# A graph kernel's edge search: gathers fetched a superblock ahead, the target list loaded alone

## The chip, the cores and the metric

The kernel runs on one core of one Trainium2 chip. The metric is device time in microseconds (us) of one execution; lower is better. The engines are named as in the profile: PE (TensorE, with PEld for its weight loads), DVE (VectorE), ACT (ScalarE), POOL (GpSimd) and SP (SyncE); a q behind a name is the engine's queue of DMA issues.

## The reference

A graph of N = 3125 nodes and E = 100,000 edges, sorted by target node `dst`, with a source `src` and one of 8 edge types. Node features `x` are 3125 x 128 in float32. Four layers follow one another, each added to its input and normalised over the features:

```python
x = _layernorm(x + gcn3(x, src, dst))                 # three GCN layers, 1/sqrt(degree) weights
x = _layernorm(x + sum_of_linear(x, src, dst))        # h[src] summed by dst, with self loops
x = _layernorm(x + gin(x, src, dst))                  # sum of neighbours, two batch norms
x = _layernorm(x + rgcn2(x, src, dst, edge_type_8))   # two layers, mean per type and target
```

Every sum over edges is a product with an adjacency matrix, in the last layer with one such matrix per edge type.

## The kernel before

The nodes are 25 blocks of 128 (`NB`), padded to 3200. The kernel first makes the dense adjacency matrix as counts, then multiplies with it. It is written in a tile framework: the program gives the operations, and a scheduler orders them on each engine when the kernel is built, adds the waits, and may bring a later operation forward into a gap. Each engine and each DMA queue then works in that order.

**Building** (`listed`, pool `f_t1`). The three edge lists are loaded as 125 x 800 (`ei`, L170). The targets are cast to float (`df`) and written back as `dsf`, 500 rows of 200. Every 200th target is loaded once more as the sample row `smp` (L173), spread over all partitions by a matmul (`smb`). Type, source and target are packed into one word per edge and stored as `pk` (L183 to L188). A superblock is 256 targets, two per partition; there are 13 (`SB`). `search(s)` counts the samples below each target (L212), gathers the row of 200 that it points to (`g`, L219, on POOL), counts in it (L224), and so has the first edge of each target (`ptr`). `keys(s)` gathers the next 64 words from there (`ew`, L234) and splits them into key columns, which PE transposes and ACT copies to `kT` (L255). `total(b)` makes block b in four units: one-hot matrices `lo` and `hi` of the keys on DVE (L161), 16 small matmuls (L271), and a cast on ACT into `at` (L273, two buffers). Then the identity is added on DVE (L277), `at` is stored as `adj_t` (L278), transposed on PE (L283), evicted by ACT to `av` (L284), stored as `adj` (L286), and summed over its rows with a column of ones (L290). The loop is

```python
search(0)
search(1)
keys(0)
for s in range(SB):
    if s + 2 < SB:
        search(s + 2)
    if s + 1 < SB:
        keys(s + 1)
    total(2 * s)
    if 2 * s + 1 < NB:
        total(2 * s + 1)
```

After it the row sums become `dinv` = 1/sqrt(degree): seven single-row copies into `rs` (L312), transposes (L314), square roots on ACT (L318 to L321), a reciprocal on DVE (L322). Sums over `at0` and `held` (L327 to L339) give the first edge of each block and a flag, `bad`.

**Layers.** With `f_t1` closed, the pool `f_nd` takes its memory. Weights, `xa` (the features) and bias rows are loaded on ACT's queue (L473 to L496). `v` = `xa` times `dinv` is split into three bfloat16 `parts` (L501 to L505), and `product` multiplies them with `adj`, read back as `m` (L514), in 525 matmuls per layer (L534); `done` applies the weight, the normalisation and the next split. Three GCN layers make 105 steps of 15 matmuls.

**The relations.** `relations` is a generator of work that `product` draws on: after each step `fill(1.3)` advances it 1.3 yields. It counts edges per type (L347, L348, eight times) into the reciprocals `inv`, gathers the edges of 11 blocks that are later treated edge by edge (`gedge`, L376), decodes them, and makes the per-type matrices of the 14 other blocks in 56 units: `rlo`, `rhq` (L161), L429, 16 matmuls (L448), casts (L455 on ACT, L457 on DVE), stores (L462). What follows, the other three layers, is not touched.

Of the kernel before, what the change touches and what calls it, by code (L numbers as in the profile page):

```python
# [8 lines left out]
F32 = mybir.dt.float32  # L9
# [63 lines left out]
def listed(ctx: ExitStack, tc: tile.TileContext, p: dict, out: bass.AP, bad):  # L73
# [11 lines left out]
    onesb = const.tile([P, 1], BF, name="onesb")  # L85
# [5 lines left out]

    def column(name, n=1):
        t = const.tile([P, n], F32, name=f"c_{name}")
        with nc.allow_non_contiguous_dma(reason="a bias"):
            nc.scalar.dma_start(t, p[name].rearrange("(n p) -> p n", p=P))
        return t
# [51 lines left out]
    with ExitStack() as lists, tc.tile_pool(name="f_ps", bufs=1, space=PSUM) as psum:  # L148
# [6 lines left out]
        begin = bg.tile([P, SB, 2], F32, name="begin")  # L155

# [9 lines left out]
        with tc.tile_pool(name="f_t1", bufs=1) as t1:  # L166

            ei = [t1.tile([EP, ET], I32, name=f"e_{n}") for n in ("dst", "src", "edge_type_8")]
            for t, name in zip(ei, ("dst", "src", "edge_type_8")):
                nc.sync.dma_start(t, p[name].rearrange("(p t) -> p t", p=EP))  # L170
            smp = t1.tile([1, 500], I32, name="smp")
            with nc.allow_non_contiguous_dma(reason="every 200th edge"):
                nc.scalar.dma_start(smp, p["dst"].rearrange("(o i j) -> o i j", o=1, j=200)[:, :, 0])  # L173
# [3 lines left out]
            smf = t1.tile([1, 500], F32, name="smf")  # L177
            nc.vector.tensor_copy(smf, smp)
            df = t1.tile([EP, ET], F32, name="df")
            nc.vector.tensor_copy(df, ei[0])  # L180
            nc.sync.dma_start(dsf.rearrange("(p a) c -> p (a c)", p=EP), df)
            w = t1.tile([EP, ET], I32, name="w0")
            nc.vector.scalar_tensor_tensor(w, ei[2], 12, ei[1], op0=OP.logical_shift_left, op1=OP.bitwise_or)  # L183
            w2 = t1.tile([EP, ET], I32, name="w1")
            nc.vector.scalar_tensor_tensor(w2, ei[0], 15, w, op0=OP.logical_shift_left, op1=OP.bitwise_or)
            none = t1.tile([GM, P], I32, name="none")
            nc.vector.memset(none, -1)
            nc.sync.dma_start(pk[:E].rearrange("(p t) o -> p (t o)", p=EP), w2)  # L188
            nc.sync.dma_start(pk[E:].rearrange("(o t) c -> o (t c)", o=GM), none)

            t = psum.tile([P, 512], F32, name="mi", tag="mi", bufs=2)
            nc.tensor.matmul(t[:, :500], ones[0:1, :], smf, start=True, stop=True)
            smb = t1.tile([P, 500], F32, name="smb")
            nc.scalar.copy(smb, t[:, :500])
# [101 lines left out]
            for s in range(SB):  # L296
                if s + 2 < SB:
                    search(s + 2)
# [1276 lines left out]
```

## Time and profile before

| | us |
|---|---|
| median of 3 runs | 2141.09 |
| lowest, highest | 2141.07, 2145.42 |
| the profiled execution | 2231.44 |
| its span, first to last instruction | 2229.5 |
| PE busy in it | 1911.2 (86%) |
| DVE busy in it | 1269.3 (57%) |
| ACT busy in it | 1056.7 (47%) |
| POOL busy in it | 900.9 (40%) |

The profile is of one execution, 4% longer than the median. The page cuts the span into 40 slices of 55.7 us and gives a digit for each, the busy share in tenths. Below, a row of a timeline has start and duration in us, engine, line, operation, output from inputs with shapes, and in brackets the idle time before it and what ended that. A row of waits has the waiting group, what it waited for, total us, number and longest. A row of windows has the stretch, its length, the busy time (and number of instructions) of PE, PEld, DVE, ACT and POOL, the clock granted to TensorE, the DMA share and GB/s.

### The profile page before, as it was taken

How to read it: one execution, taken by the hardware profiler on the slowest of the kernel's cores; microseconds unless marked ns; L12 is line 12 of the kernel's file. 1: busy time of each engine (PE TensorE's matmuls, PEld its weight loads, DVE VectorE, ACT ScalarE, POOL GpSimd, SP SyncE). 2: the span in 40 equal slices, each digit the busy share in tenths (PEclk: the TensorE clock that was granted, in tenths of full speed). 3: DMA queues.
4: the chain of work that ended last, by engine and by line, in shares of the span. 5: the costliest groups of instructions: out<-in, count | busy, mean ns of one | idle time of the engine just before them, and what ended most of it. 6: DMA issues, size and time to landing. Idle time of an engine off the chain costs nothing.

```text
span 2229.5 us, 31941 instructions
## 1 busy us (share of the span) xinstructions
PE 1911.2 (86%) x12176; PEld 1382.8 (62%) x12176; DVE 1269.3 (57%) x2303; ACT 1056.7 (47%) x1151; POOL 900.9 (40%) x898
## 2 busy tenths in 40 slices
PE   1767769999999699778998999898878998998984
PEld 0455536666665588556677667567636776777773
DVE  4888889999996563363444445344236443334333
ACT  1767744544442466542232333232327676766760
POOL 3222121221120000027657357437525766766664
PEclk9777779999999899988999999999989999999996
DMA  3444466888787788175656567446538877778762
GB/s 86 190 177 174 177 202 206 273 291 270 263 270 250 238 264 238 45 213 157 168 168 165 169 178 201 128 150 170 148 105 252 239 215 211 224 219 235 205 168 68
DMA packets 384636, 433.06 MB, mean 194 GB/s; under 512 B 28731, under 2 KB 350301, under 8 KB 384472
## 3 DMA queue, kind: packets, MB, share of 16 engines
q1 hardware_dynamic: 314318, 278.95, 40.8%
q0 software_dynamic: 45920, 119.66, 18.2%
q10 hardware_dynamic: 24234, 32.31, 5.0%
q8 instruction: 97, 1.59, 0.3%
q14 instruction: 67, 0.55, 0.1%
HBM read 319.22 MB, written 111.58 MB: 193 GB/s over the span
## 4 chain that ended last, share of the span: by engine, by line
PE 58%; DVE 17%; DMA 8%; issue 7%; ACT 4%; another core or an unknown queue 3%; POOL 2%; ACTq 0%; SPq 0%; DVEq 0%; POOLq 0%
PE acc L772 24%; PE ga L814 7%; PE acc L534 7%; PE acc L569 6%; PE mi L852 4%; PE mi L862 3%; DVE lo L161 2%; DMA g<-dsf,irow 2%; PE bld L448 2%; DVE rhq L161 2%; ACT m L767 2%; DVE hi L161 2%; DVE rlo L161 1%; DMA back<-ht_d 1%
## 5 line engine op out<-in xcount | busy, mean ns | idle before, releaser
L772 PE MATMUL acc<-m,hilo 128*128 128x384 f32 (+1 forms) x3200 | 776.2, 386 | 44.8 <-issue 28.6
L772 PEld LDWEIGHTS acc<-m,hilo 128*128 128x128 f32 x3200 | 580.4, 194 | 132.3 <-issue 53.1
L767 ACT CAST m<-m 128x2560 fp32r<-128x2560 uint8 (+1 forms) x224 | 454.7, 2061 | 438.2 <-remote 140.4
L806 POOL DMA_INDIRECT gx<-xt_d,gsrc x355 | 388.4, 1094 | 553.9 <-DMA inv<-inv_d 293.5
L806 POOL DMA_INDIRECT gx<-ht_d,gsrc x355 | 364.8, 1028 | 213.1 <-issue 77.5
L534 PE MATMUL acc<-m,parts 128*128 128x512 bf16 (+1 forms) x1575 | 333.7, 358 | 11.6 <-DMA r_L_gnn_g<-in_L_gnn_g 10.5
L814 PE MATMUL ga<-oh,gx 128*128 128x192 bf16 (+1 forms) x2442 | 264.7, 245 | 65.6 <-issue 38.1
L814 PEld LDWEIGHTS <-gx 128*128 128x128 bf16 x2442 | 178.7, 99 | 156.4 <-issue 126.5
L798 DVE TENSOR_TENSOR oh<-iota,gkey 128x768 bf16<-128x768 bf16 (+1 forms) x188 | 100.1, 533 | 263.9 <-PE ga L814 134.1
L534 PEld LDWEIGHTS <-parts 128*128 128x128 bf16 x1575 | 152.5, 98 | 135.2 <-issue 13.6
L769 DVE CAST m<-m 128x2560 fp32r<-128x2560 uint8 (+1 forms) x96 | 151.9, 1584 | 115.8 <-PE ga L814 32.2
L455 ACT CAST rb<-bld 128x800 uint16<-128x800 f32 x179 | 143.8, 829 | 124.3 <-PE bld L448 119.2
L462 POOL DMA_DIRECT2D rel<-rb x112 | 64.4, 583 | 285.3 <-ACT rb L455 181.2
L569 PE MATMUL acc<-mf,halves 128*128 128x512 f32 (+1 forms) x700 | 155.0, 379 | 16.9 <-ACT mf L566 16.7
L569 PEld LDWEIGHTS acc<-mf,halves 128*128 128x128 f32 x700 | 128.6, 191 | 37.5 <-issue 18.3
L161 DVE TENSOR_TENSOR lo<-iota,kT 128x2048 bf16<-128x2048 bf16 x100 | 121.7, 1217 | 0.0
L746 DVE TENSOR_TENSOR e<-mi,t 128x512 f32<-128x512 f32 x50 | 34.3, 687 | 137.5 <-ACT t L745 134.5
L566 ACT CAST mf<-m 128x2560 fp32r<-128x2560 bf16 (+1 forms) x42 | 88.2, 2102 | 47.9 <-PE acc L569 38.7
L271 PE MATMUL bld<-hi,lo 128*128 128x50 bf16 x1600 | 75.0, 201 | 40.0 <-DVE hi L161 24.2
L448 PE MATMUL bld<-rhq,rlo 128*128 128x200 bf16 x896 | 106.9, 252 | 1.6 <-DVE rb L457 1.0
L448 PEld LDWEIGHTS <-rlo 128*128 128x128 bf16 x896 | 82.5, 98 | 36.0 <-issue 7.6
L271 PEld LDWEIGHTS <-lo 128*128 128x128 bf16 x1600 | 64.1, 107 | 64.3 <-DVE hi L161 27.1
(230 smaller groups left out, 2093.2 us busy)
## 6 DMA issues: line engine op xcount, KB each, us to landing
m<-rel SPq DMA_DIRECT2D x160, 320.0 KB
rel<-rb POOLq DMA_DIRECT2D x112, 400.0 KB
m<-adj SPq DMA_DIRECT2D x60, 640.0 KB
m<-rel SPq DMA_DIRECT2D x160, 240.0 KB
m<-adj_t SPq DMA_DIRECT2D x40, 640.0 KB
m<-adj SPq DMA_DIRECT2D x45, 480.0 KB
adj_t<-at SPq DMA_DIRECT2D x25, 800.0 KB
adj<-av SPq DMA_DIRECT2D x25, 800.0 KB
```

The source lines that it names most:

```text
L161: nc.vector.tensor_tensor(o, (iota2 if of is None else of)[:, None, :width, :].to_broadcast([P, PU // 2, width, 2]), k[:, :, None, :].to_b ...
L271: nc.tensor.matmul(pt[:, j, : 2 * NB], lo[:, j // 2, :, j % 2], hi[:, j // 2, :, j % 2], start=True, stop=True)
L448: nc.tensor.matmul(pt[:, k, : R * NB], lo[:, j // 2, :, j % 2], hq[:, j // 2, :, j % 2], start=True, stop=True)
L455: nc.scalar.copy(o, src)
L534: nc.tensor.matmul(o, x[:, k, :], m(k - k0), start=(k == 0 and i == 0), stop=(k == NB - 1 and i == 2))
L569: nc.tensor.matmul(acc[:, :w], x[:, 5 * g + k, :], mf[:, k, :w], start=(g == 0 and k == 0 and i == 0), stop=(more is None and g == 4 and k ...
L767: nc.scalar.copy(v, src)
L769: nc.vector.tensor_copy(v, src)
L772: nc.tensor.matmul(acc[:, :w], x[:, 5 * g + k, :], m[:, k, :w], start=(g == 0 and k == 0 and i == 0), stop=(g == 4 and k == 4 and i == 1),)
L798: nc.vector.tensor_tensor(oh[:, : nt // 2], iota2[:, None, : GW * R, :].to_broadcast([P, nt // 2, GW * R, 2]), gkey[:, g, t : t + nt].rear ...
L806: nc.gpsimd.indirect_dma_start(out=gx.rearrange("p i c -> p (i c)"), out_offset=None, in_=table[:], in_offset=bass.IndirectOffsetOnAxis(ap ...
L814: nc.tensor.matmul(acc[:, a:z], gx[:, i, :], oh[:, t % 4 // 2, a - c0 : z - c0, t % 2], start=(a // 512 not in seen), stop=(t == GT[g] - 1 ...
```

## The change

- The target list is loaded first; the other two lists wait for it. The sample row is no longer loaded but made from `df`: four columns of it times the identity (`smf`), summed by a matmul with ones.
- The loads of `xa`, of all weights, rows and bias columns move from ACT's queue to SP's, wait for the store of the packed words (`later`), and, but for the columns and `xa`, lie in a pool of their own, `f_w`. The packing waits for the first superblock's coarse count.
- `search` is split: `coarse(s)` counts the samples and issues the gather of `g`; `search(s, gs)` counts in what came. `keys` is split likewise by `fetch_edges(s)`. The loop runs `coarse` three superblocks ahead, `search` and `fetch_edges` two, `keys` one.
- `total` is split: what follows the casts (`stored`) comes after the first two units of the next block.
- The row sums use a 32-column `onesb` and give 32 equal rows; three wide copies take the place of the seven single-row ones and of the clearing of `rs`, which has one buffer. An early square root on ACT brings its table in.
- `at0`, `held` and `bad` move into `relations`, followed by the gathers of `gedge`, which stood behind the counting; the counting gets a yield per type; the store of `inv_d` moves behind the decoding. `fill` has 1.4 for 1.3.

```diff
-    onesb = const.tile([P, 1], BF, name="onesb")
+    onesb = const.tile([P, 32], BF, name="onesb")
...
+    nc.scalar.activation(const.tile([P, 1], F32, name="root_eps"), eps_ln, AF.Sqrt)
+    packed = []
+    def later(ld):
+        tc.add_manual_dep(ld.ins, packed[0].ins.name, WAIT, reason="the edges come first")
...
-            nc.scalar.dma_start(t, p[name].rearrange("(n p) -> p n", p=P))
+            later(nc.sync.dma_start(t, p[name].rearrange("(n p) -> p n", p=P)))
...
+        def square(name):
+            t = wp.tile([D, D], F32, name=f"w_{name}")
+            later(nc.sync.dma_start(t, p[name]))
+            return t
+        def row(name):
+            t = wp.tile([P, D], F32, name=f"r_{name}")
+            later(nc.sync.dma_start(t, bcast(p[name], D)))
+            return t
...
+            for ld in loads[1:]:
+                tc.add_manual_dep(ld.ins, loads[0].ins.name, WAIT, reason="the targets come first")
...
-                nc.scalar.dma_start(smp, p["dst"].rearrange("(o i j) -> o i j", o=1, j=200)[:, :, 0])
...
+                for i in range(4):
+                    nc.vector.tensor_scalar(smf[:, :, i], ident[:EP, :EP], df[:, 200 * i : 200 * i + 1], None,
+                                            op0=OP.mult)
+                t = psum.tile([P, 512], F32, name="mi", tag="mi", bufs=2)
+                nc.tensor.matmul(t[:, :500], ones[:EP, :], smf.rearrange("p a i -> p (a i)"), start=True, stop=True)
+                nc.scalar.copy(smb, t[:, :500])
...
-            def search(s):
+            def coarse(s):
...
+                gs = []
                 for c in (2 * s, 2 * s + 1):
                     g = t1.tile([P, 200], F32, name="g", bufs=4)
                     nc.gpsimd.indirect_dma_start(
                         out=g, out_offset=None, in_=dsf[:],
                         in_offset=bass.IndirectOffsetOnAxis(ap=irow[:, c : c + 1], axis=0),
                     )
+                    gs.append(g)
+                return gs
+
+            def search(s, gs):
+                own = slice(2 * s, 2 * s + 2)
+                for c, g in zip((2 * s, 2 * s + 1), gs):
                     junk = t1.tile([P, 500], BF, name="junk", bufs=2)
                     nc.vector.tensor_scalar(junk[:, :200], g, nid[:, c : c + 1], 0.0, op0=OP.is_lt,
                                             op1=OP.add, accum_out=fine[:, c : c + 1])
...
-            def keys(s):
-                own = slice(2 * s, 2 * s + 2)
+            def fetch_edges(s):
                 ew = t1.tile([P, 2, SL], I32, name="ew", bufs=3)
...
+                return ew
+
+            def keys(s, ew):
+                own = slice(2 * s, 2 * s + 2)
...
-            def total(b):
+            def total(b, behind):
                 at = t1.tile([P, NB, P], BF, name="at", bufs=2)
                 for u in range(64 // PU):
+                    if u == 2 and behind is not None:
+                        stored(*behind)
...
+                return b, at
+
+            def stored(b, at):
                 nc.vector.tensor_add(at[:, b, :], at[:, b, :], identb)
                 nc.sync.dma_start(adj_t[b], at)
...
+            for s in range(-3, SB):
+                if s + 3 < SB:
+                    near[s + 3] = coarse(s + 3)
+                if 0 <= s + 2 < SB:
+                    search(s + 2, near.pop(s + 2))
+                    edges[s + 2] = fetch_edges(s + 2)
+                if 0 <= s + 1 < SB:
+                    keys(s + 1, edges.pop(s + 1))
+                for b in range(max(2 * s, 0), min(2 * s + 2, NB)):
+                    built = total(b, built)
+            stored(*built)
+
+            tc.add_manual_dep(words.ins, started[0].ins.name, WAIT, reason="the search comes first")
...
-                rs = t1.tile([P, 512], F32, name="rs", bufs=2)
-                nc.vector.memset(rs, 0.0)
-                for i in range(4 * g, min(7, 4 * g + 4)):
-                    q, w = 32 * (i % 4), min(512, NP - 512 * i)
-                    nc.scalar.copy(rs[q : q + 1, :w], row[g][q : q + 1, :w])
+                rs = t1.tile([P, 512], F32, name="rs")
+                if g == 0:
+                    nc.scalar.copy(rs, leave[0])
+                else:
+                    nc.scalar.copy(rs[:64], leave[1][:64])
+                    nc.scalar.copy(rs[64:96, :P], leave[1][64:96, :P])
...
-                        fill(1.3)
+                        fill(1.4)
```

## The prediction

> **What bounds the kernel now.** I read the page's 40 slices first. VectorE (DVE) is at 8 or 9 tenths in slices 1 to 11, the only stretch that the change touches apart from slice 0; after it TensorE (PE) leads.
>
> ```profile
> PE   1767769999999699778998999898878998998984
> DVE  4888889999996563363444445344236443334333
> ```
>
> Then the timeline gives four landmarks: first one-hot of the building stage (`lo`, L161) at 42.11 us, last one-hot (`hi`) ending at 285.04, TensorE running the layers' products (L534) without gaps from 312.96, and their end near 731. Before 42.11 the chain of waits is a row of transfers:
>
> ```profile
> 16.05 0.41 DVE L178 CAST smf<-smp 1x500 f32<-1x500 int32 x1 [13.28 <-DMA smp<-in_dst]
> ...
> 25.74 1.11 POOL L219 DMA_INDIRECT g<-dsf,irow  x1 [20.70 <-DMA dsf<-df]
> ...
> 42.11 1.22 DVE L161 TENSOR_TENSOR lo<-iota,kT 128x2048 bf16<-128x2048 bf16 x1
> ```
>
> The samples (`smp`) land at 16, the target list written back (`dsf`) at about 25.7, and the first gather needs both. For the building stage I took the busy times and the waits of DVE in that window, and one stretch at its end without gathers (columns: PE, weight load, DVE, ACT, POOL busy, then the granted clock, DMA share, GB/s):
>
> ```profile
> 42.10:285.10 243.00, 167.18 (x2372) 119.30 (x2373) 211.19 (x461) 165.65 (x302) 56.04 (x44) 0.77 0.45 172
> 333.00:690.00 357.00, 353.30 (x2338) 220.90 (x2337) 347.73 (x628) 172.12 (x249) 63.20 (x109) 1.00 0.80 264
> ```
> ```profile
> DVE junk L224 <- DMA g<-dsf,irow: 22.4, 15, 3.6
> DVE at L277 <- ACT at L273: 8.3, 19, 0.9
> ```
> ```profile
> 128.40:140.30 11.90, 7.53 (x108) 6.09 (x108) 11.72 (x20) 6.28 (x11) 2.99 (x2) 0.57 0.35 137
> 262.00:290.00 28.00, 20.01 (x361) 14.45 (x360) 26.78 (x44) 24.82 (x48) 0.00 (x0) 0.99 0.56 228
> ```
>
> DVE works 211.2 of 243 us; its 31.8 idle us are two waits: the search waits for its own gather (22.4), and the addition of the identity (L277) waits for ACT's last cast (8.3, and 0.9 unnamed). ACT (165.7) and PE (167.2) have room. So the stage is DVE plus two waits. Between the stages stands a third:
>
> ```profile
> 298.28 0.32 DVE L322 RECIPROCAL dinv<-dinv 128x25 f32<-128x25 f32 x1 [1.67 <-ACT dinv L321]
> ...
> 308.97 1.01 ACTq L485 DMA_DIRECT2D r_L_gnn_beta<-in_L_gnn_beta  x1
> ...
> 310.02 1.55 ACT L501 CAST parts<-v 128x512 bf16<-128x512 f32 x3 [11.57 <-DMA gedge<-pk,gi]
> ...
> 310.74 0.59 PE L534 MATMUL acc<-m,parts 128*128 128x512 bf16 x1 [10.49 <-DMA r_L_gnn_g<-in_L_gnn_g]
> ```
>
> The 11.57 us are put down to a gather, but ACT's own queue was issuing twelve weight and row loads from 298.97 to 309.98; the cast stands behind them.
>
> **What the Trainium skill says.** "DMA: Bandwidth & Descriptors", section Anatomy of one DMA, prices a transfer at about 2.0 us plus bytes over 436 GB/s. The gathers agree: issued at 34.22, used at 36.94. The write of `dsf` doesn't: 0.4 MB would be 2.9 us, and it took 7.9 (16.96 to 24.86) at a DMA share of about a third; the edge lists, too, have 125 rows. I use the trace. The same page, section Issuing engines are not separate DMA queues, says that moving a load to another issuer saves only sequencer time; here that time is the 11 us above. "ScalarE: Activation LUTs", section What ACT_TABLE_LOAD costs, gives 1283 ns; the trace has 1.28 us at L318. "TensorE: Matmul & The Clock Gate", section What's actually happening, says an idle window halves the clock: the trace has 0.57 at 128.4 to 140.3 and 0.99 at 262 to 290.
>
> **The change part by part.** Times as H, the end of the last `hi`.
>
> *Start.* The target list is loaded alone (the other two lists wait for it, `xa`, weights and rows wait for the packed words); `smp`, 500 separate elements, goes, and the samples come from `df` by four small DVE steps (0.2 us each by their size, near L178's row of 0.41), one matmul of 500 columns (2.03, row L192) and the copy (0.58). From 14 to 16 us, with `xa` mostly in, the core's transfers ran at 120 GB/s; I take that as the lists' own rate (an estimate), so one takes 3.4 us of transfer and lands near 6.2. Then 0.56 + 1.2 + 2.03 + 0.58 puts the samples at 10.7, and four coarse counts of 0.66 put the first rows at 13.6. `dsf` is issued near 7, but behind the two other lists (0.8 MB, 6.7 us at that rate) on SP's queue: 16 to 22; I take 19. So the first gather goes from 25.7 to 19. From there the order on POOL is four gathers, g2, two `ew`, g2, two `ew`; g2 waits for the search of superblock 1. At 1.25 us an issue and 2.7 to land (34.22 to 36.94): search 1 done at +7.2, last `ew` issued at +13.5, landed +16.2, keys of superblock 1 (1.7) before the first `lo`: +18, where it is +16.4 now. First `lo` at **37** instead of 42.1: -5. Bounds 31.5 (`dsf` in time for 13.7) and 41 (at 23).
>
> *SP's queue.* 26 loads now stand on SP between the packed words and the first `adj_t` store. They can be issued from some 25 us; 26 x 0.4 us (ACT's issues of them now: 0.33 to 0.97) plus the landing of 1.6 MB of `xa` (8 us at the 205 GB/s of 6 to 12 us; each load waits in the program for the eighth before it) ends before 45; the first store is due after six pairs of one-hots, 37 + 9.7 = 47. Cost nothing; if that cover is gone, it is ACT's third block that waits for the buffer.
>
> *Building.* `coarse` issues superblock s+3's gather before s+2 is searched, `fetch_edges` one iteration ahead of `keys`, and `stored` comes two pairs into the next block. Both DVE waits lose their cause. The counts stay, but the third coarse count, search 2 and keys 1 (4.4 us) are done before the first `lo`: 211.2 - 4.4 = 206.8. What is late next: the `at` buffer (two) is now stored half a block later, so ACT's first cast of block b+2 waits for the landing of b's store: issued, then four more pairs of DVE and PE work when no search lies between (6 us), against 800 KB, at the busy rate (3.2 MB in 45% of 20.2 us, 2.3 us each) plus 2 to 3: 4.3 to 6. And PE at the low clock needs per block 4 x 0.86 + 25 x 0.12 + 6.3 x 0.59 = 10.2 us, warm 4 x 0.58 + 25 x 0.07 + 6.3 x 0.38 = 6.5; DVE asks one per 8.5. Warm it fits; cold it would be busy throughout, and in 262 to 290 a busy share of 71% already goes with 0.99. I put 9 us (0.8 a superblock) for both, bounds 0 and 22. The 32-column `onesb` costs PE at most the difference of weight loads, 0.10 against 0.08 us, x175 = 3.5, beside DVE. H = 37 + 206.8 + 9 = 252.8 against 285.04: **-32**, the start included.
>
> *Between the stages.* Now H + 27.9 for gapless L534. The last casts and evictions (H + 6.4) stay. Seven one-row copies (6 x 0.59 + 0.26) become three (0.58, 0.58, 0.27), the table load (1.28) has moved to the idle start; a single `rs` gives some back: -2.5 at the reciprocal. `at0` and `held` leave the pool, so the first `m` load no longer waits for their matmul (6.4 us on SP). One `cnt` reduction (1.88) stays in front of `v` on DVE. Without the twelve loads ACT casts at once; the limit is now `m`: issued near H + 11, 640 KB in 4 us, H + 15; gapless two later: H + 17.5: **-10** (bounds -6, -12).
>
> *Layers.* PE is 99% busy, DVE 97%. The edge gathers (11 on POOL, 1.4 us each) move ahead of the counting; DVE waits 1.3 us for them at L381 now, so at most that is gained; POOL has nothing else due. `inv_d`'s store moves behind the decoding, needed hundreds of us later. The merged `iv` copy saves 0.4. The generator has ten more yields and rate 1.4: done after 128/1.4 = 91 steps of 105, as 118/1.3 now. But two counts (4.9 us) move into a full DVE, and in the new PE order the units lie between the 210th and 1380th L534 instead of 139th and 1365th: 56 x 0.19 = 11 us less PE cover for the same DVE work, against 9 of slack: **+4** (bounds -1, +15).
>
> Sum: -32 - 10 + 4 = **-38** on the profiled execution's 2231.44, so 2193; the median of the runs is 2141.09, 4% less, and the same ratio gives 2104. Extremes: -62 (2082) and -7 (2134).
>
> **The rivals.** (a) The forecast, all three gains, 0.74. (b) PE becomes the bound of building by staying at the low clock: 25 x 10.2 = 255, H = 292, total +7 - 10 + 4: 2232, **2142**, no change. For it: 0.77 now; against it: 0.99 at a PE share of 71% in 262 to 290. 0.04. (c) DVE starves PE in the layers by the whole 11 + 5 and a like amount from the normalisations queued behind the one-hots: +25, so -17, **2125**. For it, DVE's 97%; against it, 40 us of plain products after the last unit. 0.12. (d) Slower: ACT's first cast waits for the `adj_t` store. The loop over two blocks is landing time L plus 9.5 us of pairs, cast and addition; beyond L = 10.7 it is longer than 20.2, and from about 12 it eats the start and the -10 too; at L = 15 it is 24.5 x 12 = 294 instead of 243: +51 - 5 - 10 + 4 = +40, **2179**. For it, `dsf` at 7.9 us for half the bytes; against it, 128 rows and a share of 0.45. 0.06. (e) The loads' order doesn't change what lands when (the lists are as late): first `lo` at 42, -33, **2109**, inside (a). Left: 0.04 better than 2078.
>
> **The numbers.** The likeliest is 2104. Range 2078 to 2132: (a), (c) and (e) with the bounds of the terms. No change means within 0.2%, about what a measurement of this kernel can tell: 0.04; slower 0.06; faster 0.90.
>
> **What would show it.** First `lo` near 37 and the first gather near 19; no DVE wait on `g`; superblocks of 17.4 to 18.2 us where they are 20.2; ACT casting `parts` within 3 us of the reciprocal; gapless products 18 us after the last `hi`; from there to the end the same within 5 us. It is wrong if superblocks stay near 20, with ACT waiting for a store or PE's clock near 0.6, or if PE waits in the layers for one-hots.

## The result, and the profile after

The changed kernel takes 2126.75 us (median of 6 runs, 2122.28 to 2130.2), the kernel before 2144.95 beside it (6 runs). The ratio is 0.9915 (95% interval 0.9898 to 0.9933): 18 us faster, where 37 were forecast. Measured again with the experiments (c0 below) it was 0.9940 (0.9922 to 0.9959). So the direction was right and less than half of the gain came.

The profiled execution of the kernel before (2231.44) was 4% above its runs, that of the changed kernel (2126.84) is like its runs. The two traces can be compared up to the end of the layers, at some 730 us; the last section says what lies behind it.

The slices of the page show DVE full to slice 12 (53 us each, 56 before) and PE leading after it, so each stage is led by the same engine as before:

```profile
PE   1667689999999699967999999999888999999994
DVE  4999888999998464263535345525434544444432
```

Four landmarks from the timelines (first `lo`; H, the end of the last `hi`; the layers' products without gaps; end of the last product):

| | first `lo` | H | gapless products | last product |
|---|---|---|---|---|
| before | 42.11 | 285.04 | 312.96 | 729.96 |
| forecast | 37 | 252.8 | 270.3 | 691 |
| after | 47.07 | 271.05 | 287.82 | 710.43 |

By stage: start +5 (forecast -5), building 242.9 to 224.0, -19 (forecast -27), between the stages 27.9 to 16.8, -11 (forecast -10), layers 417.0 to 422.6, +5.6 (forecast +4). The sum is -19.5, about what the timed runs show. The start and the building stage are where 18 us are missing.

**Start.** The timeline of the changed kernel (start, duration, engine, line, operation, output and input, in brackets the idle time and what ended it):

```profile
19.36 1.11 POOL L259 DMA_INDIRECT g<-dsf,irow  x1 [14.32 <-DMA dsf<-df]
...
33.97 0.94 POOL L279 DMA_INDIRECT ew<-pk,ptr  x1 [0.30 <-DMA g<-dsf,irow]
...
35.22 0.94 POOL L279 DMA_INDIRECT ew<-pk,ptr  x1 [0.30 <-issue]
...
45.37 0.23 DVE L288 TENSOR_SCALAR f<-ew 128x128 int32<-128x128 int32 x1 [5.19 <-DMA ew<-pk,ptr]
...
47.07 1.22 DVE L183 TENSOR_TENSOR lo<-iota,kT 128x2048 bf16<-128x2048 bf16 x1
```

The first gather starts 0.4 us from its forecast. But the edges (`ew`) of superblock 1, issued at 33.97 and 35.22, are used at 45.37: ten microseconds to land, where 2.7 had been put down.

**Building.** The windows of the changed kernel for building and for the time to gapless products (columns as in the prediction), and then DVE's waits in the first of them:

```profile
47.07:271.05 223.98, 151.81 (x2381) 112.58 (x2381) 205.75 (x439) 160.31 (x299) 131.67 (x40) 0.82 0.48 185
271.05:287.82 16.77, 9.96 (x81) 5.60 (x78) 15.08 (x24) 10.90 (x27) 4.48 (x4) 0.78 0.68 241
```
```profile
DVE f L288 <- DMA ew<-pk,ptr: 12.5, 7, 3.5
DVE junk L270 <- DMA g<-dsf,irow: 5.7, 4, 3.2
```

DVE works 205.75 us (forecast 206.8) and waits 18.2, all of it for late gathers. POOL's 131.67 us are new: before, 56 us in a stage 19 us longer. The group on the page and one gather in the timeline tell why (g: 988 ns in the median before, 1887 at most):

```profile
L259 POOL DMA_INDIRECT g<-dsf,irow x26 | 78.1, 3003 | 79.3 <-DVE fine L272 51.5
```
```profile
81.54 14.28 POOL L259 DMA_INDIRECT g<-dsf,irow  x1 [0.30 <-issue]
81.68 1.22 DVE L183 TENSOR_TENSOR lo<-iota,kT 128x2048 bf16<-128x2048 bf16 x1
...
94.42 0.58 DVE L183 TENSOR_TENSOR hi<-iota,kT 128x800 bf16<-128x800 bf16 x1
94.90 0.73 DVE L251 TENSOR_SCALAR_CACHE_REDUCE junk<-smb,nid 128x500 bf16<-128x500 f32 x1
...
96.12 0.94 POOL L279 DMA_INDIRECT ew<-pk,ptr  x1 [0.30 <-issue]
```

A gather that starts just ahead of the first `lo` stays on POOL for 14.28 us, as long as DVE does nothing but one-hots and the two additions, and ends 0.92 us after DVE begins its next count (L251). Seven of 52 gathers last 13.6 to 14.3 us. Four of them fetch `g` and three `ew`. What stands behind them on POOL is issued late, lands late, and DVE waits some 3 us in the next superblock.

**Between the stages**, in the timeline, the cast follows `v` and the products follow `m`:

```profile
281.15 0.32 DVE L383 RECIPROCAL dinv<-dinv 128x25 f32<-128x25 f32 x1 [0.63 <-ACT dinv L382]
...
284.71 1.57 ACT L540 CAST parts<-v 128x512 bf16<-128x512 f32 x3 [3.09 <-DVE v L633]
...
286.07 0.59 PE L573 MATMUL acc<-m,parts 128*128 128x512 bf16 x1 [2.93 <-DMA m<-adj]
...
287.82 1.46 PE L573 MATMUL acc<-m,parts 128*128 128x512 bf16 x3 [0.28 <-DVE parts L544]
```

**Layers.** The longest wait of PE between 290 and 740 us, apart from the known one behind the layers (L608), is new:

```profile
PE mi L476 <- DVE gs L474: 4.7, 1, 4.7
```

### The profile page after: what moved, and what is told of

It reads as the page before. It is cut to its first block, busy times and chain, and to the rows that moved or that the text cites. A ratio compares the mean times of both kernels' runs of the same rounds, so it can differ in the third digit from the quotient of the medians.

```text
span 2125.0 us, 31949 instructions
## 1 busy us (share of the span) xinstructions
PE 1860.9 (88%) x12176; PEld 1355.6 (64%) x12176; DVE 1265.8 (60%) x2303; ACT 1052.8 (50%) x1146; POOL 983.0 (46%) x898
## 5 line engine op out<-in xcount | busy, mean ns | idle before, releaser
L811 PE MATMUL acc<-m,hilo 128*128 128x384 f32 (+1 forms) x3200 | 747.7, 379 | 21.5 <-issue 15.3
L811 PEld LDWEIGHTS acc<-m,hilo 128*128 128x128 f32 x3200 | 567.7, 190 | 87.9 <-issue 21.4
L853 PEld LDWEIGHTS <-gx 128*128 128x128 bf16 x2442 | 171.1, 98 | 163.4 <-issue 67.4
L608 PE MATMUL acc<-mf,halves 128*128 128x512 f32 (+1 forms) x700 | 155.0, 379 | 16.0 <-ACT mf L605 15.9
L608 PEld LDWEIGHTS acc<-mf,halves 128*128 128x128 f32 x700 | 128.9, 191 | 36.3 <-issue 17.5
L259 POOL DMA_INDIRECT g<-dsf,irow x26 | 78.1, 3003 | 79.3 <-DVE fine L272 51.5
L183 DVE TENSOR_TENSOR rhq<-iota,kT 128x3200 bf16<-128x3200 bf16 x56 | 101.7, 1816 | 0.0
```

The lines of the kernel that those rows point to most:

```text
L183: nc.vector.tensor_tensor(o, (iota2 if of is None else of)[:, None, :width, :].to_broadcast([P, PU // 2, width, 2]), k[:, :, None, :].to_b ...
L608: nc.tensor.matmul(acc[:, :w], x[:, 5 * g + k, :], mf[:, k, :w], start=(g == 0 and k == 0 and i == 0), stop=(more is None and g == 4 and k ...
L811: nc.tensor.matmul(acc[:, :w], x[:, 5 * g + k, :], m[:, k, :w], start=(g == 0 and k == 0 and i == 0), stop=(g == 4 and k == 4 and i == 1),)
L853: nc.tensor.matmul(acc[:, a:z], gx[:, i, :], oh[:, t % 4 // 2, a - c0 : z - c0, t % 2], start=(a // 512 not in seen), stop=(t == GT[g] - 1 ...
```

## The experiments

The theory after this reading: (1) the first edge gathers are late because of the loads that now stand beside them; (2) gathers are held on POOL while DVE runs its steps with two inputs in SBUF (one-hots and additions); (3) PE waits for one sum in the layers. Rivals: POOL's own order at the start; the stores' traffic as the cause of late gathers; a phase between POOL and DVE; DVE's load in the layers. No experiment leaves out any of the computation. Each was timed beside the kernel before on the same chip; ratios are to that. The chips differ in the part of the program behind these stages (last section), so ratios from different chips compare only roughly. The landmarks are those of one profiled execution each, with the first product in place of the gapless ones.

| | ratio (interval) | first `lo` | H | first product | last product starts |
|---|---|---|---|---|---|
| c0 after again | 0.9940 (0.9922 to 0.9959) | 46.3 | 271.1 | 285.5 | 709.8 |
| e1 loads late | 0.9891 (0.9865 to 0.9916) | 37.9 | 263.8 | 278.8 | 702.7 |
| e13 features early | 0.9919 (0.9892 to 0.9947) | 37.4 | 264.0 | 278.9 | 702.8 |
| e2 tiny counts | 0.9928 (0.9904 to 0.9952) | 47.4 | 267.8 | 282.3 | 705.2 |
| e9 long counts | 0.9916 (0.9896 to 0.9936) | 46.4 | 269.1 | 283.3 | 706.1 |
| e12 tiny in the run | 0.9867 (0.9837 to 0.9897) | 46.1 | 252.5 | 267.2 | 691.5 |
| e5 POOL delay | 0.9930 (0.9914 to 0.9945) | 45.6 | 268.5 | 282.9 | 708.5 |
| e3 keys between | 0.9852 (0.9825 to 0.9879) | 46.0 | 251.2 | 267.6 | 693.2 |
| e8 split undone | 1.0027 (1.0012 to 1.0041) | 39.1 | 294.0 | 308.2 | 732.2 |
| e6 counts first | 0.9952 (0.9937 to 0.9967) | 42.8 | 268.8 | 283.2 | 715.8 |
| e4 loads late, keys between | 0.9797 (0.9769 to 0.9825) | 36.8 | 241.9 | 257.1 | 682.5 |
| e7 that, product later | 0.9779 (0.9764 to 0.9794) | 36.2 | 241.2 | 255.9 | 677.0 |
| e10 e7, loads at the casts | 0.9786 (0.9767 to 0.9805) | 36.7 | 241.7 | 261.8 | 680.5 |
| e11 e7, stored at once | 0.9827 (0.9810 to 0.9844) | 36.3 | 256.6 | 272.1 | 693.2 |

### The changed kernel again

No edit.

> The changed kernel itself, as the measure for the others on this chip: ratio to the kernel before 0.990 to 0.993, first one-hot at 47, last hi at 271, gapless products from 288, products of the layers until 710, several gathers held 13 to 14 us on POOL.

All as expected but the ratio, 0.9940, which lies above the range: seven gathers of 13.6 to 14.5 us, and 19.2 us of DVE waits for g and `ew` in the building stage (18.2 in the first profile).

### The start: which transfers are in the way

```diff
     def later(ld):
-        tc.add_manual_dep(ld.ins, packed[0].ins.name, WAIT, reason="the edges come first")
+        held_back.append(ld)
...
             stored(*built)
+            for i, ld in enumerate(held_back):
+                tc.add_manual_dep(ld.ins, added[i // 3].ins.name, WAIT, reason="after the first blocks")
```

> The changed kernel, but the features, weights and rows (26 loads) wait for the first additions of the identity, three loads for each block, instead of for the packed words. Theory: the edge gathers of superblocks 0 and 1 land 6 to 10 us after their issue because those loads fill the DMA engines and stand in the same stretch; without them a gather lands about 2.7 us after its issue, the first one-hot goes from 47 to 37 or 38 us and the kernel from 2127 to about 2118. Rival: the gathers come late because of POOL's own order and the searches in front of them; then the first one-hot stays at 44 or later and the time within 3 us of 2127. A second rival: the loads now stand in front of the first stores on SP's queue, ACT waits for the store of block 0, and what is won at the start is lost by the third block (2125 or more).

First `lo` 37.9. H is 7 us earlier than in the changed kernel; the held gathers stay (seven over 10 us, 19.4 us of waits in the building stage). The second `ew` of superblock 1 now lands in 2.9 us; in the two traces of the changed kernel and six more whose loads are early it took 7.8 to 10.6. Held back are the weights, rows and columns as well as the features. In the second version the big load of features keeps its early place:

```diff
-            later(nc.sync.dma_start(
-                xa[:, : NB - 1, :], p["x"][: (NB - 1) * P].rearrange("(b p) d -> p b d", p=P)
-            ))
+            big = nc.sync.dma_start(
+                xa[:, : NB - 1, :], p["x"][: (NB - 1) * P].rearrange("(b p) d -> p b d", p=P)
+            )
+            tc.add_manual_dep(big.ins, packed[0].ins.name, WAIT, reason="the edges come first")
```

> The changed kernel with weights and rows after the first blocks, but the features (1.6 MB, one load) behind the packed words as in the changed kernel. It tells which of the loads delays the first edge gathers. If it is the features' bytes, the first one-hot stays at 44 to 47 us; if it is the many small loads of weights and rows, it goes to 37 to 39 as it did with all of them moved; 41 would be a share of each.

First `lo` 37.4: the features' 1.6 MB do not delay it, the 24 small loads (weights, rows, columns and the last 53 rows of features) do. Windows of six microseconds, first of the changed kernel, then of e13 (the last three columns are granted clock, DMA share, GB/s):

```profile
24.00:30.00 6.00, 0.00 (x0) 0.00 (x0) 3.75 (x20) 0.00 (x0) 1.17 (x2) 1.00 0.89 244
30.00:36.00 6.00, 0.00 (x0) 0.00 (x0) 0.87 (x7) 0.00 (x0) 4.56 (x5) 1.00 0.72 140
36.00:42.00 6.00, 0.69 (x3) 0.31 (x3) 2.08 (x11) 0.48 (x1) 2.05 (x3) 1.00 0.60 79
```
```profile
24.00:30.00 6.00, 0.00 (x0) 0.00 (x0) 4.14 (x22) 0.00 (x0) 2.35 (x3) 1.00 0.90 257
30.00:36.00 6.00, 0.69 (x3) 0.31 (x3) 2.74 (x16) 0.48 (x1) 4.48 (x6) 1.00 0.30 80
36.00:42.00 6.00, 2.35 (x35) 1.89 (x35) 6.00 (x16) 1.66 (x3) 5.70 (x2) 1.00 0.12 34
```

The features pass in 24 to 30 in both, at a share of 0.9. They do slow a gather in their midst: in e13 one issued at 27.04 is used at 32.42, where e1 has 26.94 and 29.53, but the first `lo` waits for a later `ew`. From 36 to 42 the changed kernel's DMA engines are busy to 0.60 at only 79 GB/s: little moved for the time taken, and this is where `ew` of superblock 1 is under way. e1 and e13 start and end the building stage alike (37.9 and 37.4, 263.8 and 264.0), so the small loads alone make the delay of the first `lo`; the times of e13 and c0 don't resolve it. What in them holds the gathers (packets, order in an engine) wasn't tried.

### The held gathers: the run of two-input steps

```diff
                     one_hot(hi, 1, b, u, 2 * NB, iota50)
+                    tiny = t1.tile([P, 3], F32, name="tiny", bufs=2)
+                    nc.vector.tensor_scalar(tiny[:, :2], nid[:, :2], 0.0, 0.0, op0=OP.is_lt, op1=OP.add,
+                                            accum_out=tiny[:, 2:3])
```

> The changed kernel with one tiny counting step (two elements a partition, one SBUF input, with an accumulator) after each hi, 100 in all; nothing is left out. Theory: a gather's issue on POOL that meets an unbroken run of one-hots (both inputs in SBUF) is held until DVE runs something else; so no gather lasts over 2.5 us on POOL (7 of them last 13.6 to 14.3 now), DVE's 18.2 us of waits for g and ew in the building stage fall below 4, and the 100 steps at 0.1 to 0.2 us each cost 10 to 20 us again: about the same time, 2120 to 2132. Rival: the gathers are late because of the DMA queues' other traffic (the stores of adj_t and adj); then the waits stay near 18 us and the time rises by the steps' whole cost, to 2137 to 2147.

Five gathers were still held for 13.7 to 14.3 us. But the trace shows that nearly all tiny counts, which depend on nothing late, had been ordered ahead of the stage and not into its runs, so this said little. Where some were left, after 215 us, the hold is short; the timeline of e2:

```profile
215.24 2.66 POOL L259 DMA_INDIRECT g<-dsf,irow  x1 [0.30 <-issue]
...
217.00 0.14 DVE L321 TENSOR_SCALAR_CACHE_REDUCE tiny<-nid 128x2 f32<-128x2 f32 x1
```

2.66 us of hold, ended 0.9 us after the tiny count's start. (The next expectation, and that of e5 below, take it from e2 that tiny counts don't end a hold; its trace doesn't show that.) The next try used longer counts:

```diff
+                    if u == 1:
+                        long = t1.tile([P, 501], F32, name="long", bufs=2)
+                        nc.vector.tensor_scalar(long[:, :500], smb[:, :500], nid[:, :1], 0.0, op0=OP.is_lt,
+                                                op1=OP.add, accum_out=long[:, 500:501])
```

> The changed kernel with a count of 500 samples (one SBUF input, 0.65 us on DVE, result not used) after the second pair of one-hots of each block, 25 in all. The tiny counts of 0.1 us didn't end a hold, and every hold ends 0.9 us after the start of the next superblock's first count, which takes 0.65 us. Theory: what ends a hold is that DVE stays off its two-input steps long enough; then a held gather ends at the first long count, no hold is over 5 us, the waits for g and ew fall from 18 to 27 us to below 8, and with 25 x 0.66 = 17 us of added counts the time is 2 us below to 8 us above that of the changed kernel. Rival: the hold has nothing to do with DVE's steps (it ends with something that the next superblock brings); then holds of 13 to 14 us stay and the time rises by 15 to 18 us.

These, too, were partly ordered ahead, which makes the run its own control. In the runs without a long count four gathers were held for 13.6 to 14.5 us; in those with one, six were held, for 3.7 to 4.3, each ending 0.9 us after the long count began. The timeline of e9:

```profile
140.35 4.28 POOL L259 DMA_INDIRECT g<-dsf,irow  x1 [0.30 <-issue]
...
143.73 0.72 DVE L322 TENSOR_SCALAR_CACHE_REDUCE long<-smb,nid 128x500 f32<-128x500 f32 x1
```

To tell a short step from a long one, 25 tiny counts were tied into the runs (`hot` lists the one-hots made so far):

```diff
+                    if u == 1:
+                        tiny = t1.tile([P, 3], F32, name="tiny", bufs=2)
+                        step = nc.vector.tensor_scalar(tiny[:, :2], nid[:, :2], 0.0, 0.0, op0=OP.is_lt, op1=OP.add,
+                                                       accum_out=tiny[:, 2:3])
+                        tc.add_manual_dep(step.ins, hot[-1].ins.name, WAIT, reason="inside the run")
```

> The changed kernel with one tiny count (two elements a partition, one SBUF input, result not used) after the second pair of one-hots of each block, each made to wait for a one-hot of that pair, so that it stands inside the run; in the earlier try with tiny counts nearly all of them had run before the stage began. 25 steps of about 0.1 us cost 2 to 4 us. Theory: a held gather is released by the first DVE step that is not a one-hot or an addition, however short; holds last at most 4.5 us (3.4 us of pairs, then 0.9), the waits for g and ew in the building stage fall from 18 to 27 us to below 8, and the ratio to the kernel before is 0.984 to 0.989 where the changed kernel had 0.9915 and 0.9940. Rival: only a step of 0.65 us or a stop of DVE releases it; then holds of 13 to 14 us stay and the ratio is 0.993 or more.

Timeline and window of e12:

```profile
63.09 4.42 POOL L261 DMA_INDIRECT g<-dsf,irow  x1 [0.30 <-issue]
63.23 1.21 DVE L185 TENSOR_TENSOR lo<-iota,kT 128x2048 bf16<-128x2048 bf16 x1
...
66.61 0.14 DVE L324 TENSOR_SCALAR_CACHE_REDUCE tiny<-nid 128x2 f32<-128x2 f32 x1
...
67.81 0.94 POOL L281 DMA_INDIRECT ew<-pk,ptr  x1 [0.30 <-issue]
```
```profile
46.10:252.50 206.40, 147.98 (x2382) 110.07 (x2381) 206.40 (x489) 161.49 (x299) 75.13 (x40) 0.87 0.52 201
```

Nine gathers are held for 4.41 or 4.42 us and one for 3.87, each ending 0.8 to 0.9 us after the tiny count; none longer. DVE then works 206.40 of 206.40 us: not one wait is left in the building stage, and the last `hi` ends at 252.5 instead of 271. Adding 25 steps that compute nothing took 18 us out of the stage. The ratio, 0.9867, is in the range expected. The stores are the same, at 201 GB/s against 185, so the rival of the stores' traffic falls: the waits are gone beside it.

So a count, even one of 0.14 us, releases the gather. A stop of DVE does too. In the changed kernel the last hold ends 0.8 us after DVE ran out of work and stood waiting for that very `ew`:

```profile
233.06 13.74 POOL L279 DMA_INDIRECT ew<-pk,ptr  x1 [0.30 <-issue]
...
245.40 0.58 DVE L183 TENSOR_TENSOR hi<-iota,kT 128x800 bf16<-128x800 bf16 x1
...
249.45 0.23 DVE L288 TENSOR_SCALAR f<-ew 128x128 int32<-128x128 int32 x1 [3.46 <-DMA ew<-pk,ptr]
```

Of the 84 holds over 2.2 us in all traces 73 end about 0.9 us after a count began, ten about 0.8 us after DVE fell idle, and one (e13, at 115.45) at neither. Not every step of another kind releases, though: e11, below, has holds that outlast the steps of `keys`. The theory stands in so far as a run on DVE holds the gather; that two inputs in SBUF are what makes a step hold it was not tried.

### POOL's phase

```diff
                 for c in (2 * s, 2 * s + 1):
+                    if c % 2 and s >= 3:
+                        idle = t1.tile([P, 374], F32, name="idle", bufs=2)
+                        it0 = nc.gpsimd.iota(idle, pattern=[[1, 374]], ...)
+                        tc.add_manual_dep(it0.ins, started[-1].ins.name, WAIT, reason="between the gathers")
                     g = t1.tile([P, 200], F32, name="g", bufs=4)
```

> The changed kernel with more work on POOL: from the fourth superblock on an iota of 374 numbers (0.63 us on POOL, its result is used by nothing) stands between or ahead of the two gathers of g. The tiny breaks after each hi did not end the holds, so an unbroken run is not the whole cause. What the tables of starts show is a matter of phase: gathers that start 0.15 us ahead of the first lo of a run are held to its end, those that start 0.35 to 0.7 us inside a lo pass when that lo ends. Theory of the phase: with the iota the second g starts 0.4 to 0.8 us inside the first lo, passes in 1.3 to 1.7 us, at most two gathers are held over 3 us where seven were, the waits for g and ew in the building stage fall from 18 to below 8, and the time falls by 8 to 14 us against the changed kernel, by adding work. Rival (DVE's run holds whichever gather it meets, and how many it holds depends on how many are still due): as many are held, the waits stay at 16 to 20 and the time is the same or up to 5 us longer.

Seven are held as before, 13.6 to 14.5 us, and the time is unchanged (0.9930 beside 0.9940). The delay was too short for the test it was meant for: the second gather now starts 0.19 us inside the first `lo`, not 0.4 to 0.8. So a start there is caught as well. Which gathers are caught stays partly open: in all traces those that start 0.5 us or more inside a `lo` pass when it ends, those 0.15 us ahead of the first one don't, and between -0.15 and +0.45 there are both.

### Keys between the blocks

```diff
-                if 0 <= s + 1 < SB:
-                    keys(s + 1, edges.pop(s + 1))
                 for b in range(max(2 * s, 0), min(2 * s + 2, NB)):
                     built = total(b, built)
+                    if b % 2 == 0 and s + 1 < SB:
+                        keys(s + 1, edges.pop(s + 1))
+                if s == -1:
+                    keys(0, edges.pop(0))
```

> The changed kernel, but the keys of the next superblock are made between its two blocks instead of ahead of both, so a run of one-hots is half as long (about 7 us) and the edge gathers have half a superblock more to land. Theory of the held gathers: none lasts over about 7.5 us, the waits for g and ew in the building stage fall from 18.2 to below 5, the last hi ends 13 us earlier (near 258) and the time is about 2114. Rival (DMA traffic): the waits fall a little, to 10 to 15, and the time stays above 2120. Rival (DVE isn't the bound: PE or ACT behind it): the waits for gathers go and others take their place; 2122 to 2127.

No gather lasts over 2 us, where holds of up to 7.5 were expected: with this order those that meet the one-hots start 0.09 to 0.72 us inside a `lo` and pass at its end. So the halved run itself was not put to the test, and that starts at 0.09 and 0.36 pass here is part of what stays open. H falls by 20 us to 251.2 and the ratio to 0.9852. It needs no added step.

### What the ahead-fetching and the deferred stores are worth

```diff
-                if s + 3 < SB:
-                    near[s + 3] = coarse(s + 3)
                 if 0 <= s + 2 < SB:
-                    search(s + 2, near.pop(s + 2))
-                    edges[s + 2] = fetch_edges(s + 2)
+                    search(s + 2, coarse(s + 2))
                 if 0 <= s + 1 < SB:
-                    keys(s + 1, edges.pop(s + 1))
+                    keys(s + 1, fetch_edges(s + 1))
```

> The changed kernel with the ahead-fetching alone undone: each search makes its own gather of g and waits for it, and the edges are fetched in front of their keys as in the kernel before; the start, the deferred stores, the loads and the layers stay as changed. Theory: the split took away 22 us of waits for g and brought back 18 to 27 of waits for late g and ew, so undoing it costs little: waits for g and ew together 20 to 28 in the building stage, ratio 0.994 to 0.998 (the changed kernel had 0.9940 and 0.9915). Rival: the split did bring what was forecast and the loss is elsewhere; then undoing it costs 15 us or more, ratio above 1.000.

The rival was right: 1.0027, H at 294.0. DVE's waits there, from 36 to 285 us:

```profile
DVE junk L270 <- DMA g<-dsf,irow: 24.4, 19, 3.8
DVE f L288 <- DMA ew<-pk,ptr: 21.8, 6, 6.6
```

The waits for g are back at the size that the prediction had for them, and the holds (four of 10.5 us) come on top. (The first `lo` there is early, but the first `hi` comes at 47.6 only.) So the ahead-fetching is worth 23 us of H even with its held gathers. With the deferral undone in the last version (e7 below):

```diff
-                    built = total(b, built)
+                    stored(*total(b, None))
...
-            stored(*built)
```

> The best version so far (ratio 0.9779), but each block's identity is added and the block stored at once instead of two pairs into the next block. Theory: DVE waits 0.4 us at most every block for ACT's last casts again (the kernel before had 9.2 us of it, 19 waits of up to 0.9): last hi 8 to 10 us later, ratio 0.9815 to 0.9830. Rival: the deferral was not needed, since the keys between the blocks give ACT the same time; then only every second block waits, 4 to 5 us, ratio 0.980.

H +15 and ratio +0.005, but not by the expected wait. DVE's waits of e11 in the same window:

```profile
DVE junk L271 <- DMA g<-dsf,irow: 10.7, 5, 3.7
DVE at L332 <- ACT at L325: 2.8, 3, 1.1
```

The addition waits 2.8 us; most of the rest is gathers caught again (six for 11.9 to 13.5 us), as the steps' order had shifted. That the ratio falls in the expected range, 0.9815 to 0.9830, is luck. One of the six in the timeline of e11:

```profile
72.91 13.49 POOL L260 DMA_INDIRECT g<-dsf,irow  x1 [0.30 <-issue]
...
77.32 0.22 DVE L289 TENSOR_SCALAR f<-ew 128x128 int32<-128x128 int32 x1
...
85.49 0.73 DVE L252 TENSOR_SCALAR_CACHE_REDUCE junk<-smb,nid 128x500 bf16<-128x500 f32 x1
```

All six last through the nine steps of `keys` (L289 to L299), four of which, like L289, have one input and no accumulator, and end at the next count or stop of DVE.

### The layers: one small product in TensorE's order

The third part of the change undone, but for `at0`, `held` and `bad`, which stay in `relations`:

```diff
-            lines = bg.tile([P, 1], F32, name="lines")
-            ... (the gathers of gedge)
             cnt = bg.tile([P, NC2, R + 1], F32, name="cnt")
             ... (counts, inv, iv, store of inv_n)
+            ... (transposes of iv, store of inv_d)
+            lines = bg.tile([P, 1], F32, name="lines")
+            ... (the gathers of gedge)
...
-                        fill(1.4)
+                        fill(1.3)
```

> The changed kernel with the third part undone: counting, the reciprocals and the store of inv_d first, then the gathers of the gathered blocks' edges, and filling at 1.3. Theory: the layers take 5 to 6 us more than before because TensorE, in its order, comes to the small product of gs 4.7 us before DVE has the sum; DVE has the counts, the decoding and the normalisations to do and can't reach it. With the counts first, that product comes later in TensorE's order and the wait goes: products end 4 to 5 us earlier and the time falls by 4 to 5 us against the changed kernel. Rival: the layers are longer because the two extra counts and the relations' pace leave TensorE without cover for DVE; then the wait shows at another product and the time is within 2 us.

Wrong: from first to last product it takes 432.6 us, 8 more than c0 (424.4). PE meets another operand that isn't there, in e6's waits of PE:

```profile
PE mi L425 <- DVE iv L419: 13.7, 1, 13.7
```

Behind it, DVE itself stood 12.06 us in the midst of the counts, waiting for the edges (`gedge`) of the late gathers. So putting the gathers first is worth 8 us against this order; the kernel before, whose order e6 does not restore in full, takes 418.8 from first to last product. What costs is a small product that PE reaches ahead of its sum. The last version has loads late, keys between, and that product tied behind later ones:

```diff
             nc.vector.tensor_reduce(gs, gw, axis=AX.XY, op=OP.add)
+            yield    # four of these
             t = psum.tile([P, 512], F32, name="mi", tag="mi", bufs=2)
-            nc.tensor.matmul(t[:, :1], ones, gs, start=True, stop=True)
+            mm = nc.tensor.matmul(t[:, :1], ones, gs, start=True, stop=True)
+            tc.add_manual_dep(mm.ins, latest[0].ins.name, WAIT, reason="behind the products so far")
```

> Loads after the first blocks, keys between the blocks, and the small product of gs ten products later in TensorE's order. The version with the first two gave a ratio of 0.9797 to the kernel before. Theory: the wait of 4.2 us for gs falls below 1 and the ratio is 0.9775 to 0.9785. Rival: TensorE waits as long at the next product that needs DVE (the transposes of iv, the first one-hots of the relations); ratio 0.9795 or more.

The ratio is 0.9779, and first to last product take 421.1 us (e4: 425.4), so by the landmarks the product's place is worth 4 us; the ratios don't resolve it. A wait of 2.5 us is left where below 1 was expected. Its building window has no gap for DVE, as in e12:

```profile
36.20:241.30 205.10, 147.98 (x2385) 109.97 (x2385) 205.10 (x445) 162.67 (x301) 59.20 (x41) 0.88 0.57 216
```

### Loads late and keys between, together

The edits of e1 and e3.

> Both: the loads after the first blocks and the keys between the blocks. If the two losses are separate, the gains add: 9 and 13 us, first one-hot near 37, last hi near 249, and about 2105, which is what the prediction had for the change itself. If they are one loss seen twice, or if something else becomes the bound of the building stage, 2113 or more.

First `lo` 36.8, H 241.9, 29 us before the changed kernel: the two losses are separate and the gains add (7 and 20 alone). With the product later (e7), on one chip, 2089.75 us stand against 2124.98 for the changed kernel and 2138.63 for the one before; this beats both.

### The loads between the stages

```diff
-            later(nc.sync.dma_start(t, p[name]))
+            if name.startswith("L0"):
+                behind.append(nc.scalar.dma_start(t, p[name]))
...
+            rec = nc.vector.reciprocal(dinv, dinv)
+            for ld in behind:
+                tc.add_manual_dep(ld.ins, rec.ins.name, WAIT, reason="at the casts")
```

> The best version so far (loads after the first blocks, keys between the blocks, product of gs later; ratio 0.9779), but the twelve weights and rows of the first layers are loaded on ACT's queue behind the reciprocal, as in the kernel before. Theory: twelve loads at 0.9 us stand in front of ACT's first cast and delay the layers by all of it: gapless products 27 us after the last hi instead of 17, and 10 us more in all (ratio 0.9822 to 0.9832). Rival: the products wait for m anyway, and ACT's queue costs 4 us at most (ratio 0.980 or less).

The first product comes 20.0 us after H, 14.7 in e7: 5.4, half of what was expected and more than the rival's 4; 3.6 are left at the last product, and the ratio doesn't resolve it. In e10 PE's wait for the first cast is

```profile
PE acc L594 <- ACT parts L561: 7.8, 1, 7.8
```

where 2.2 us of it are there without the loads.

## Why the prediction was half right

**Start, -5 forecast, +5 measured.** The list alone, the samples (10.9 for 10.7), the first rows (13.6) and the first gather (19.36 for 19) were right. The step that failed is the +18 from there: each gather was given 2.7 us to land, a price from a quiet stretch. It came to +27.7: the last `ew` took 10.1 us to land, and it was issued at +15.9, not +13.5, because a `g` of superblock 1 had taken 4.9. The loads that the change sets beside these gathers (26 in the prediction, 27 in the trace) were costed only for what is queued behind them on SP (and there rightly: 25 were issued by 46.40, and the first store, at 57.04, had not to wait). That their transfers run beside POOL's gathers was not counted. Without the small ones the +18 is +18.3 (19.1 to 37.4 in e13).

**Building, -27 forecast, -19 measured.** DVE's work was right (205.75 for 206.8). The 9 us for PE's low clock and the `at` buffer were not needed: DVE waits for neither, ACT waits 0.9 us once for a store, and the clock stayed at 0.82. "Both DVE waits lose their cause" is the step that failed: the search no longer waits for its own gather, but gathers were counted at 1.25 us of POOL wherever they stand, and 18.2 us of waits came for those held, for 13.6 to 14.3 us, behind one-hots. Where DVE waits for no gather the stage takes 205 to 206 us, less than the 215.8 forecast (e7, e12).

The Trainium skill has the means to suspect it: "SBUF — State Buffer", section Who interferes with whom, says that a DVE instruction with two SBUF inputs contends with a GpSimd instruction that reads SBUF, and its Summary: rules for kernel authors that the second to issue is blocked until the first finishes. The gathers that pass at a `lo`'s end (1.3 to 2 us) fit it, and so does the release by a count, which has one input in SBUF. Two things differ. The hold outlasted the instruction and went through up to 18 of them, 14.28 us. And the same section infers that a `tensor_tensor` does not stall a DMA from POOL, while the one-hots, which are such instructions, do. That the shared interface is the cause is the page's reading; the runs show the steps.

**Between the stages, -10 forecast, -11 measured** (H + 16.8 for H + 17.5). The casts come 3.6 us after the reciprocal for 3 expected. But the twelve loads, put at 11 us ahead of the cast, are worth 5.4 by e10; the rest may be the shorter row sums, the moved table load and the earlier `m`, which were not tried singly.

**Layers, +4 forecast, +5.6 measured.** The size was near, the cause another. Rival (c), DVE short of time, is right in so far as PE waits for it; but it is one wait of 4.7 us for `gs`, in PE's order, and not lost cover for the one-hots. Its total, 2125, is near the measured 2126.75 by luck: the 18 us were lost in the start and in building. The gain put on the earlier edge gathers, 1.3 us of DVE's wait for them at most, did not come either; DVE waits 3.8 us for them (L439).

**The rivals.** (b), PE cold, and (d), the store in ACT's way, did not happen. (e), loads' order without effect, had the first `lo` at 42; it came at 47, worse than any case that had been thought of, since the mechanism was missing.

## What to carry to other kernels

When a load is moved, ask not only who stands behind it on its queue but which transfers of other queues it will run beside, and take a landing time from a stretch that is as busy. When a wait on the busiest engine is taken away, ask what the other engines will then run into: here the new order ran gathers issued by POOL into unbroken runs of one-hots, which could hold one for their whole length. The order of the steps, or one count of 0.14 us in each block, brought 18 to 20 us of H beside the 23 of fetching ahead.

## What the runs showed of the hardware that was not expected

- A gather's issue on POOL, 0.94 us alone, lasted up to 15.06 us (e1, e6) beside an unbroken run of DVE steps with two inputs in SBUF. In 83 of 84 holds it ended 0.8 to 0.9 us after a count began, even one of 0.14 us (e12), or after DVE fell idle. One-input steps without an accumulator, four of 0.22 us in a row, did not end it (e11).
- Beside small loads (weights and rows of 64 KB of SBUF each, columns of 128 numbers) a gather took 7.8 to 10.6 us to land, at a DMA share of 0.60 and 79 GB/s in the changed kernel; with them moved away it took 2.4 to 2.9 (e13, e1). A load of 1.6 MB at about 250 GB/s stretched one gather from 2.6 to 5.4 us.
- The kernel before takes 2138.63 and 2140.95 us on two chips and 2251.28 and 2251.39 on two others, each with all its runs close together. e4 on one of the latter and e7 on one of the former agree to 6 us up to the last product, and the rest of the program takes 1520 and 1408 us. In the traces of the result it is 1500 us before the change and 1415 after it. So the 4% by which the profile of the kernel before exceeded its runs lie behind the stages of this case, for the most part.
